# Layer 1: the q and k projections of images 2 to 7 as three one-pass products, with the blocks around the feed-forward in another order

## The chip, the cores and the metric

The kernel runs on one core of a Trainium2 chip. The metric is device time in microseconds (us) of one launch, weights and inputs in device memory; lower is better. TensorE (PE) multiplies matrices into PSUM, VectorE (DVE) and ScalarE (ACT) evict and transform, GpSimd (POOL) does small statistics, SyncE (SP) issues nearly all transfers.

## What is computed

The reference, cut to what matters, for 8 images of 384 channels and 32x32 = 1024 tokens:

```python
# layer 0
x = x + _L0_conv_ref(_gn(x), ...)            # group norm, 8-head attention with a relative bias
# layer 1
t = _to_tokens(x)
t = t + _L1_attn_ref(_ln_t(t), qkv_w, proj_w, proj_b)
t = t + _L1_ffn_ref(_ln_t(t), W1, b1, W2, b2)

def _L1_attn_ref(x, qkv_w, proj_w, proj_b):
    qkv = (x @ qkv_w.T).reshape(B, N, 3, H, D).transpose(2, 0, 3, 1, 4)   # H = 6, D = 64
    q, k, v = qkv[0], qkv[1], qkv[2]
    q, k = _normalize(q), _normalize(k)      # mean and deviation over the 64 of a head
    attn = softmax(q @ k.T * scale)
    return (attn @ v) ... @ proj_w.T + proj_b
```

The feed-forward has weights reduced to signs around a group mean and an 8-bit scale from the largest absolute value of an image; by its grouping only images 0 to 4 get one. Everything is float32.

## The kernel before, in words

The work is written out by hand in the order in which each engine is to do it (`tc.manual_schedule()`); nothing reorders it. Every engine works through its own list in order, and SP issues transfers in order, waiting at the head of its list for whatever the next transfer needs. `later.after(n, work)` puts work off by n calls of `later.step()`.

**Layer 0** (`_layer0`) goes image by image: 32 units of attention (`scores`, `weigh`), then the projections of the next image. Those of images 1 to 7 are already done in the manner that the change takes to layer 1: `cut_weights` (L511) cuts the weights into a high part (upper mantissa bits), a low part and a mix of both, stores them in device memory, and `Ahead.project` (L581) multiplies each part in one pass (type fp32r): high x high and low x low add up in one PSUM tile (`pg`), mixed x mixed fills a second (`pm`); ACT and DVE then combine the two into q or k. A block is one (pair of heads, q or k); there are six, and each is 18 matmuls of 128x512.

**Layer 1** (`_layer1`) goes image by image: 24 units of attention (`scores` L1486, `weigh` L1535), then the rest. Images 0 to 4 have a feed-forward, and there the six q/k projections of the next image (`project_qk`, L1342: six float32 matmuls, one PSUM tile, one DVE copy L1350 or L1352, one ACT square L1358) stand between its parts as work for PE while other engines are busy. The order around image b's feed-forward is: value projections 0, 1, 2 of the next image (`project_v`, L1423), between them the last two units' `weigh`; `project_out` (L1632, residual L1640); block 0 with the token sums in its middle (`token_sums` L1309); block 1; block 2; head sums of pair 0 (`head_sums` L1371); block 3; `feed_forward_1` (y1p, L1727) with the head sums of pair 1; block 4; block 5; value projection 3; `feed_forward_2` (y2p, L1778) with the head sums of pair 2.

Three chains run beside this. (1) The layer norm (`layer_norm`): token sums, `trf` copy, four small transfers and POOL steps, broadcasts `lc` and `ls`, then on DVE scale (L1671), shift (L1674), on ACT the cast to the high part (L1675), on DVE the low part `lun` (L1679), for three chunks k. (2) The normalisation of q and k (`normalise_qk`): a small transfer `hc`, a power on POOL (L1392), `hi`, `kc`, and some steps later the broadcasts `rq` and a DVE multiply (L1413). (3) The scale of the feed-forward: the maxima of the twelve y1 tiles on DVE (L1714), an all-reduce, `quant_scale`, then gelu (L1758), `hy` (L1766) and `ly` (L1767), which feed y2p.

Images 5 and 6 have no feed-forward; there `attention_inputs` does the six blocks, the head sums, and the four value projections in one go.

PSUM is one pool of four tiles of 128x1024 (`mm2`, tag "p"). A tile is handed on when the engine that reads it has passed that reading instruction. The pool "w" of layer 1 has 16 tiles of 128x1024 in SBUF.

Of the kernel before, what the change touches and what calls it, by code (L numbers as in the profile page):

```python
# [19 lines left out]
F32 = mybir.dt.float32  # L20
# [7 lines left out]
P = 128  # L28
# [72 lines left out]

class _Shared:
# [23 lines left out]
class _Weights:  # L126
# [4 lines left out]
    def __init__(self, tc, ins, ready, shared):  # L131
        self.nc, self.ins, self.ready, self.shared = tc.nc, ins, ready, shared

# [39 lines left out]
    def store(self):  # L173
        self.nc.sync.dma_start(self.ready, self.w.rearrange("p k c -> p (k c)"))

# [17 lines left out]
def _layer0(tc, ins, x1, sums, shared, weights, beside):  # L193
# [9 lines left out]
    with ExitStack() as ctx:  # L203
# [298 lines left out]
        blocks = [(pair, s) for pair in range(NF0) for s in range(2)]  # L502
        BB = len(blocks) // 2
        cut = dram.tile([len(blocks), P, 3, KC, P], F32, tag="cut", name="cut", bufs=1)

        def masked(out, of):

            nc.vector.tensor_single_scalar(
                out.bitcast(INT), of.bitcast(INT), MASK, op=ALU.bitwise_and
            )  # L510

        def cut_weights(k):


            w = plain[:, ts(k, 2 * C)]
            high, low = etile(f"ch{k}")[:, 0 : 2 * C], etile(f"cl{k}")[:, 0 : 2 * C]
            parts = [etile(f"c{i}_{k}", dtype=F32R)[:, 0 : 2 * C] for i in range(3)]
            masked(high, w)
            nc.scalar.copy(parts[0], high)
            nc.vector.tensor_sub(low, w, high)  # L520
            nc.vector.tensor_scalar_mul(parts[1], low, CUT)
            nc.vector.scalar_tensor_tensor(parts[2], low, -CUT, high, ALU.mult, ALU.add)
            for i, part in enumerate(parts):
                nc.sync.dma_start(
                    cut[:, :, i, k].rearrange("n p c -> p n c"),
                    part.bitcast(F32).rearrange("p (n c) -> p n c", c=P),
                )

        class Cut:


            def __init__(self):
                t = shared.pool.tile([P, KC * 3 * C], F32R, tag="w", name="wc")
                self.w = t.rearrange("p (n i k c) -> p n i k c", n=BB, i=3, k=KC)

            def load(self, n):
                pair, s = blocks[n]
                nc.sync.dma_start(
                    self.w[:, n % BB].rearrange("p i k c -> p (i k c)").bitcast(F32),
                    cut[s * NF0 + pair].rearrange("p i k c -> p (i k c)"),  # L540
                )

        class Ahead:
# [16 lines left out]
            def mask(self, k):  # L560
                masked(self.high(k), self.xn[:, k])
# [13 lines left out]
            def mixed(self, k):  # L575
                t = etile(f"xd{self.b}_{k}", dtype=F32R)
                nc.vector.scalar_tensor_tensor(
                    t, self.parts[1][k].bitcast(F32), -CUT, self.high(k), ALU.mult, ALU.add
                )
                self.parts[2].append(t)  # L580

            def project(self, weights, n):
                pair, s = blocks[n]
                t = self.tile(pair)[:, s]
                name = f"{self.b}_{pair}_{s}"
                ps = mm2("pg" + name), mm2("pm" + name)
                for i in range(3):
                    for k in range(KC):
                        for h in range(NH):
                            nc.tensor.matmul(  # L590
                                ps[i // 2][:, h], weights.w[:, n % BB, i, k],
                                self.parts[i][k][:, ts(h, HALF)],
                                start=(k == 0 and i != 1), stop=(k == KC - 1 and i != 0),
                            )
                by = D0**-0.5 if s == 0 else 1.0
                nc.scalar.activation(  # L596
                    t, flat2(ps[1]), AF.Identity, scale=-by / CUT,
                    bias=bq[:, pair : pair + 1] if s == 0 else bqk[:, s, pair : pair + 1],
                )
                nc.vector.scalar_tensor_tensor(  # L600
                    t, flat2(ps[0]), by * (1.0 + 1.0 / CUT), t, ALU.mult, ALU.add
                )
                last = self.tile(NF0)
                for j in range(2):
                    nc.sync.dma_start(
                        last[j * S0 + pair * FR : j * S0 + (pair + 1) * FR, s],
                        t[j * S0 + D0 : (j + 1) * S0],
                    )
                later.step()
# [194 lines left out]
        for k in range(KC):  # L804
            later.after(18 + 3 * k, lambda k=k: cut_weights(k))
        for b in range(B):
            held = []
            for i, u in enumerate(units):
# [15 lines left out]
                if i == 26 and b == 0:  # L824
                    weights_qk = Cut()
                    for n in range(BB):
                        weights_qk.load(n)
# [14 lines left out]
            order = [n % len(blocks) for n in range(b % 2 * BB, b % 2 * BB + len(blocks))]  # L842

            def project(some):
                for n in some:
                    ahead.project(weights_qk, n)
                    if n in order[:BB]:
                        weights_qk.load((n + BB) % len(blocks))
# [346 lines left out]
def _layer1(tc, ins, x1, out, shared, start, before=None, check=None):  # L1195
# [4 lines left out]
    with ExitStack() as ctx:  # L1200
# [14 lines left out]
        def wtile(name, shape=(P, N)):  # L1215
            return work.tile(list(shape), F32, tag="w", name=name)
# [42 lines left out]

        tiny = const.tile([P, 2], F32, tag="tiny", name="tiny")  # L1260
# [8 lines left out]
        v = const.tile([P, MT, C], F32, tag="v", name="v")  # L1269

# [94 lines left out]

        def head_sums(b, pair, sq, d):
# [51 lines left out]
        def project_v(b, xt, m2, c=None, copy=nc.vector.tensor_copy):  # L1418

            pv = mm2(f"pv{b}_{m2}")  # L1420
            for i in range(2):
                for k in range(KC):
# [3 lines left out]
                        wqkv[:, k, 2 * C : 3 * C], start=(k == 0), stop=(k == KC - 1),  # L1426
# [228 lines left out]
        def layer_norm(b, xt, c):  # L1655
# [30 lines left out]
            def finish():  # L1686
                for k in range(1, KC):
                    scaled(k)
                    low(k - 1)
                    shifted(k)  # L1690
                low(KC - 1)
# [125 lines left out]
        def attention_inputs(b, xt, rest=(), sums=None):  # L1817
# [12 lines left out]
            for pair in range(NP1):  # L1830
                for s in range(2):
                    project_qk(b, pair, s, xt, qk, sq)
                    if (pair, s) == (0, 1):
                        token_stats(f"a{b}", tk)
                    if s == 0 and pair > 0:
                        head(pair - 1, *((3, 3) if pair == 1 else (5, 4)))
            for work in rest:
                work()
                later.step()
# [12 lines left out]
        for name, weights, shape, at, totals, means, signs in (  # L1852
# [6 lines left out]
            for g in range(NG):  # L1859
                later.after(totals[g], lambda g=g, stages=stages: stages[1](g))  # L1860
                later.after(signs[g], lambda g=g, stages=stages: stages[3](g))
        later.after(1, rest_of_pools)
        qk, kc = attention_inputs(0, xt)
        behind = None
        for b in range(B):
# [9 lines left out]
            for i, u in enumerate(units):  # L1875
# [7 lines left out]
                if i == 3:  # L1883
# [5 lines left out]
                    if more:  # L1889
                        *ahead_sums, stages = fold(f"a{b + 1}", ahead)  # L1890
                        for at, stage in zip((13, 14, 15, 19, 20), stages):
                            later.after(at - i, stage)
            if not more:
# [6 lines left out]
            if not ffn:  # L1900

                def last(i, b=b, oT=oT, held=held):
# [5 lines left out]
                    b + 1, ahead, [lambda: last(0), lambda: last(1)], ahead_sums  # L1908
# [4 lines left out]
            else:  # L1913
                nqk, sq, d, nkc = {}, {}, head_rows(b + 1), kc_tile(b + 1)

                def project(pair, s, step=True, middle=None):
                    return project_qk(b + 1, pair, s, ahead, nqk, sq, step, middle)
# [4 lines left out]
                for i in range(2):  # L1922
                    project_v(b + 1, ahead, i)
                    weigh_last(b, oT, held[i])
                divide(b, oT, [NP1 - 1], (1, 1))
                project_v(b + 1, ahead, 2)
                fsq, fc = [], []
                project_out(b, oT, xt, lambda m, _: fsq.append(square(f"f{b}", xt, m)), later.step)
                two = wtile(f"two{b}")
                nc.vector.tensor_add(two, xt[:, 0], xt[:, 1])  # L1930
                nc.vector.tensor_add(fsq[0], fsq[0], fsq[1])
                project(
                    0, 0,
# [4 lines left out]
                )  # L1938
                tk = fc[1]
                un, begin, normal = layer_norm(b, xt, fc[0])  # L1940
                project(0, 1)
                take = project(1, 0, step=False)
# [4 lines left out]
                take = project(1, 1, step=False)  # L1947
                normal()
                take()

                def between_1(m):
                    if m == 2:
                        normalise(0, 5, 2)
                    elif m == 4:
                        head_sums(b + 1, 1, sq, d)
                        normalise(1, 5, 3)

                y1, top = feed_forward_1(b, un, between_1)
                project(2, 0)
# [3 lines left out]
                supply.gelu(1)  # L1963
                supply.split(0)
                project(2, 1, step=False)()
# [4 lines left out]
                def between_2(k):  # L1970
                    if k == 0:
# [12 lines left out]
def tile_conv_attn_hybrid(ctx: ExitStack, tc: tile.TileContext, ins, out):  # L1984
    dram = ctx.enter_context(tc.tile_pool(name="x1", bufs=1, space=DRAM))
    x1 = dram.tile([B, C, N], F32, tag="x1", name="x1")
    ready = dram.tile([P, KC * 3 * C], F32, tag="ready", name="ready")
    state = ctx.enter_context(tc.tile_pool(name="state", bufs=1))
    flag = state.tile([P, 1], mybir.dt.int32, tag="flag", name="flag")
    sums = state.tile([P, B, NP0, 2 * N // P], F32, tag="sums", name="sums")  # L1990
    with ExitStack() as main, tc.manual_schedule():
# [3 lines left out]
            tc, ins, x1, sums, shared, _Weights(tc, ins, ready, shared),  # L1995
# [3 lines left out]
            tc, ins, x1, out, shared, start, before,  # L1999
# [4 lines left out]
    with tc.If(out_of_range > 0):  # L2004
        _layer0_shifted(tc, ins, x1)
        with ExitStack() as again, tc.manual_schedule():
# [4 lines left out]
            _layer1(tc, ins, x1, out, shared, start)  # L2011
# [44 lines left out]
```

## Time and profile before

| what | value |
|---|---|
| device time, three runs | 3014.68, 3003.15, 3005.71 us; median 3005.71 |
| the profiled execution's own time | 3006.06 us |
| its span in the profile | 3004.1 us |
| mean granted PE clock | 0.999 |
| layer 0 / layer 1, by the start of layer 1's first sums | to 1402.6 us / from there |
| one image of layer 1 with a feed-forward (2, as an example) | 1912.3 to 2136.7 us |
| one image without | 2723.8 to 2878.0 us |

How to read it: the span is the time between the first and the last instruction in the trace. Busy shares are of that span. In the view of waits a row says which instruction of an engine waited for which other, us in total, times, and the longest. The timeline gives start, duration, engine, line and tile, and in brackets the idle time of that engine before the instruction with what ended it. A float32 matmul is recorded as two instructions.

### The profile page before, as it was taken

The page shows a single profiled execution, that of the slowest core. Times are in us where ns is not written, and L with a number is a line of the kernel's source. Part 1 is how long each engine was busy: PE and PEld are TensorE (multiplying, and loading weights), DVE is VectorE, ACT ScalarE, POOL GpSimd, SP SyncE. Part 2 cuts the span into 40 slices and gives each one's busy share as a digit, 9 for nine tenths or more (in the row PEclk, how much of TensorE's full clock was granted, in tenths as well). Part 3 has the DMA queues.
Part 4 walks back from the last instruction along what each step waited for, and adds up shares of the span by engine and source line. Part 5 has one row for each costly group of instructions (what it writes and reads, how often), then busy time and mean ns, then how long its engine had stood idle before and what let it go on. Part 6 is the DMA issues. An engine that isn't in the chain of part 4 may idle for free.

```text
span 3004.1 us, 46389 instructions
## 1 busy us (share of the span) xinstructions
PE 2974.7 (99%) x19154; PEld 1640.6 (55%) x19154; DVE 1871.5 (62%) x1861; ACT 1447.9 (48%) x1802; POOL 469.4 (16%) x315
## 2 busy tenths in 40 slices
PE   8999999999999999999999999999999999999999
PEld 3355656656565656644546656656656656645453
DVE  3775747575665747564655755755755755755546
ACT  2653626354553626353553643643644643654534
POOL 3120202121110202112202202202202202211110
PEclk9999999999999999999999999999999999999999
DMA  7533030312213030223301101101101101102011
GB/s 201 147 104 93 23 110 17 96 37 51 76 30 97 23 111 17 75 81 97 77 23 31 51 23 31 51 23 31 51 23 31 51 23 31 51 17 72 17 52 38
DMA packets 114285, 171.22 MB, mean 57 GB/s; under 512 B 60848, under 2 KB 71328, under 8 KB 113712
## 3 DMA queue, kind: packets, MB, share of 16 engines
q1 hardware_dynamic: 110800, 166.33, 19.3%
q8 instruction: 154, 2.52, 0.4%
q10 hardware_dynamic: 3264, 1.82, 0.2%
q14 instruction: 67, 0.55, 0.1%
HBM read 126.44 MB, written 32.61 MB: 53 GB/s over the span
## 4 chain that ended last, share of the span: by engine, by line
PE 90%; DVE 4%; DMA 3%; SPq 2%; ACT 1%; issue 1%; POOL 1%; DVEq 0%; ACTq 0%; POOLq 0%
PE o L673 14%; PE s L642 14%; PE s L1486 11%; PE o L1535 11%; PE y2p L1778 6%; PE pq L1342 5%; PE pp L737 4%; PE pv L1423 4%; PE y1p L1727 4%; PE pp L1632 4%; PE pg L590 4%; PE pv L616 4%; PE pm L590 2%; SPq L403 1%; DVE e L653 1%; PE sum L1562 1%
## 5 line engine op out<-in xcount | busy, mean ns | idle before, releaser
L653 DVE TENSOR_TENSOR e<-s,grow 128x1024 f32<-128x1024 f32 x512 | 600.9, 1217 | 167.8 <-PE s L642 167.5
L657 ACT ACTIVATE e<-e 128x1024 f32<-128x1024 f32 x512 | 535.6, 1057 | 337.9 <-DVE e L653 317.4
L642 PE MATMUL s<-qk 48*64 48x512 f32 x4096 | 610.6, 593 | 9.9 <-DVE e L653 9.4
L673 PE MATMUL o<-e,v 64*64 64x512 f32 x4096 | 603.7, 590 | 0.9 <-DVE e L653 0.9
L1497 ACT ACTIVATE e<-s,kc 128x512 f32<-128x512 f32 x768 | 463.9, 694 | 170.8 <-PE s L1486 160.3
L1486 PE MATMUL s<-qk,qk 64*64 64x512 f32 x3072 | 418.3, 592 | 0.3
L1535 PE MATMUL o<-e,v 64*64 64x512 f32 x3072 | 414.8, 590 | 0.0
L642 PEld LDWEIGHTS s<-qk 48*64 48x64 f32 x4096 | 234.9, 132 | 242.5 <-issue 93.7
L673 PEld LDWEIGHTS o<-e,v 64*64 64x64 f32 x4096 | 250.1, 133 | 189.8 <-issue 99.0
L1512 DVE TENSOR_TENSOR t<-t,e 128x1024 f32<-128x1024 f32 x192 | 230.9, 1221 | 54.0 <-ACT e L1497 53.9
L1486 PEld LDWEIGHTS s<-qk,qk 64*64 64x64 f32 x3072 | 153.5, 132 | 190.1 <-issue 109.5
L1342 PE MATMUL pq<-bx,wqkv 128*128 128x512 f32 x576 | 254.1, 595 | 0.7 <-ACT tra L1314 0.7
L1535 PEld LDWEIGHTS o<-e,v 64*64 64x64 f32 x3072 | 157.6, 133 | 171.1 <-issue 143.8
L702 POOL TENSOR_TENSOR inv<-sums,over 128x16 f32<-128x16 f32 x32 | 93.4, 2917 | 891.7 <-DMA sums<-sd 749.0
L1342 PEld LDWEIGHTS pq<-bx,wqkv 128*128 128x128 f32 x576 | 107.8, 190 | 143.5 <-issue 139.7
L1509 DVE TENSOR_TENSOR t<-e,e 128x1024 f32<-128x1024 f32 x96 | 114.2, 1224 | 81.5 <-ACT e L1497 81.4
L1714 DVE TENSOR_REDUCE parts<-y 128x1 f32<-128x1024 f32 x75 | 90.1, 1217 | 94.4 <-ACT y L1711 93.9
L1358 ACT ACTIVATE qsq<-pq 128x1024 f32<-128x1024 f32 x48 | 49.2, 1025 | 190.6 <-DVE qk L1352 101.9
L1392 POOL TENSOR_TENSOR hc<-hc,rsqrt 128x32 f32<-128x32 f32 x24 | 138.5, 5772 | 2.0
L1423 PE MATMUL pv<-wqkv,bx 128*128 128x384 f32 x384 | 131.9, 497 | 0.0
L600 DVE SCALAR_TENSOR_TENSOR qk<-pg,qk 128x1024 f32<-128x1024 f32 x42 | 51.4, 1225 | 128.2 <-ACT qk L596 128.2
L1423 PEld LDWEIGHTS pv<-wqkv,bx 128*128 128x128 f32 x384 | 119.1, 315 | 19.0 <-issue 9.7
(185 smaller groups left out, 3298.3 us busy)
## 6 DMA issues: line engine op xcount, KB each, us to landing
rb<-rd SPq DMA_DIRECT2D x110, 256.0 KB
wc<-cut SPq DMA_DIRECT2D x24, 576.0 KB
xn<-in_x_dram SPq DMA_DIRECT2D x24, 512.0 KB
res<-in_x_dram SPq DMA_DIRECT2D x24, 512.0 KB
x<-res SPq DMA_DIRECT2D x24, 512.0 KB
bx<-x SPq DMA_DIRECT2D x8, 1536.0 KB
rq<-hi SPq DMA_DIRECT2D x48, 256.0 KB
out_dram<-bx SPq DMA_DIRECT2D x23, 512.0 KB
```

The costliest lines, as they stand in the source:

```text
L590: nc.tensor.matmul(ps[i // 2][:, h], weights.w[:, n % BB, i, k], self.parts[i][k][:, ts(h, HALF)], start=(k == 0 and i != 1), stop=(k == K ...
L642: nc.tensor.matmul(s[j][ts(c, QP), i], qk[pair][rows, 1, ts(4 * m2 + 2 * i + c, QP)], qk[pair][rows, 0, ts(h, HALF)], start=True, stop=True,)
L653: nc.vector.tensor_add(e.rearrange("p (i q) -> p i q", i=2), s[j], bass.AP(near.tensor, near.offset, [near.ap[0], [-QROWS * IW, 2], [1, HA ...
L657: nc.scalar.activation(e, e, AF.Exp)
L673: nc.tensor.matmul(po[ts(j, S0), r], v[keys, 2 * m2 + i, 2 * pair + j, :], es[j][keys, ts(i, HALF)], start=(m2 == 0 and i == 0), stop=(m2 ...
L1342: nc.tensor.matmul(pq[:, h], wqkv[:, k, s * C + pair * P : s * C + (pair + 1) * P], xt[:, k, ts(h, HALF)], start=(k == 0), stop=(k == KC - 1),
L1423: nc.tensor.matmul(pv[:, i, 0:C], xt[:, k].rearrange("c (p m) -> c m p", m=MT)[:, 2 * m2 + i], wqkv[:, k, 2 * C : 3 * C], start=(k == 0), ...
L1486: nc.tensor.matmul(s[j][ts(c, QP), i], qk[pair, 1][rows, ts(4 * m2 + 2 * i + c, QP)], qk[pair, 0][rows, ts(h, HALF)], start=True, stop=True,)
L1497: nc.scalar.activation(e[:, ts(i, HALF)], s[j][:, i], AF.Exp, scale=kc[:, pair, j, m : m + 1])
L1512: nc.vector.tensor_add(total[j], total[j], e)
L1535: nc.tensor.matmul(po[ts(j, D1), r], v[keys, 2 * m2 + i, at : at + D1], es[j][keys, ts(i, HALF)], start=(m2 == 0 and i == 0), stop=(m2 == ...
L1778: nc.tensor.matmul(py[m][:, h], w2[:, k, ts(m, P)], supply.parts[k][i][:, ts(h, HALF)], start=(k == 0 and i == 0), stop=(k == FC - 1 and i ...
```

## The change

Layer 1 gets the cut products for images 2 to 7. The helpers of layer 0 move to the top of the file. The weights of layer 1 are cut during image 1 of layer 0 (units 17 to 26) and kept in device memory. Image 1 of layer 1 keeps the float32 products. For images 2 to 7 the high, low and mixed parts of the normalised input are made on DVE and ACT during the attention units of the image before and kept in the room of the feed-forward's second weight, `w2`, which is stored once and loaded again for each feed-forward. Weight blocks go through four slots; blocks 4 and 5 are loaded into the slots of 0 and 1. A block writes two PSUM tiles and its mixed product comes first, except for the first block of an image. Layer 0's blocks after the first of an image also take the mixed product first.

Around the feed-forward the order for b = 1 to 4 becomes: value projection 0; the last two `weigh`; block 0; `project_out`; block 1 with the token sums; blocks 2 and 3; head sums of pair 0; blocks 4 and 5; `feed_forward_1` with the head sums of pairs 1 and 2; value projections 1, 2, 3; `feed_forward_2`. The weight of the value projections has a tile of its own (`wv`).

The diff, cut to its core (helpers that only moved are left out):

```diff
+    def products(self, n, i, out, part):
+        w = self.slots[n % len(self.slots)].rearrange("p (i k c) -> p i k c", i=3, k=KC)
+        for k in range(KC):
+            for h in range(NH):
+                self.nc.tensor.matmul(
+                    out[:, h], w[:, i, k], part[k][:, ts(h, HALF)],
+                    start=(k == 0 and i != 1), stop=(k == KC - 1 and i != 0),
+                )
...
+                if b == 1 and i in (17, 20, 23):
+                    k = (i - 17) // 3
+                    t = etile(f"cw{k}")[:, 0 : 2 * C]
+                    weights.load_part(k, t)
+                    later.after(3, lambda k=k, t=t: weights.cut(k, t, *cut_tiles(f"1{k}")))
...
-                    ahead.project(weights_qk, n)
+                    ahead.project(cuts, n, (0, 1, 2) if n == order[0] else (2, 0, 1))
...
+        def project_cut(b, n, parts, dst, sq, step=True, middle=None, order=(2, 0, 1)):
+            pair, s = BLOCKS[n]
+            name = f"{b}_{pair}_{s}"
+            ps = mm2("pg" + name), mm2("pm" + name)
+            for at, i in enumerate(order):
+                if middle is not None and at == 2:
+                    middle()
+                cuts.products(n, i, ps[i // 2], (parts.high, parts.low, parts.mixed)[i])
+            def take():
+                t = qkp.tile([P, N], F32, tag="qk", name="qk" + name)
+                to = t if s == 0 else t.rearrange("c (m p) -> c p m", m=MT)
...
+                nc.scalar.activation(to, of[1], AF.Identity, scale=-1.0 / CUT)
+                nc.vector.scalar_tensor_tensor(to, of[0], 1.0 + 1.0 / CUT, to, ALU.mult, ALU.add)
+                q = wtile("qsq" + name)
+                nc.scalar.activation(
+                    q if s == 0 else q.rearrange("c (p m) -> c p m", m=MT), to, AF.Square
+                )
...
+                        cuts.load(0)
+                        cuts.load(1)
+                        parts = Parts(b + 1, ahead)
+                        for k, at in enumerate((8, 10, 12)):
+                            later.after(at - i, lambda k=k, parts=parts: parts.cut_high(k))
+                        for k, at in enumerate((16, 17, 18)[: 1 if ffn else KC]):
+                            later.after(at - i, lambda k=k, parts=parts: parts.cut_low(k))
+                        for k, at in enumerate(() if ffn else (19, 21, 22)):
+                            later.after(at - i, lambda k=k, parts=parts: parts.mix(k))
...
+                else:
+                    project_v(b + 1, ahead, 0)
+                    weigh_last(b, oT, held[0])
+                    for k in range(1, KC):
+                        parts.cut_low(k)
+                    weigh_last(b, oT, held[1])
+                    divide(b, oT, [NP1 - 1], (1, 1))
+                    for k in range(KC):
+                        parts.mix(k)
+                    project(0, order=(0, 1, 2))
                 fsq, fc = [], []
                 project_out(b, oT, xt, lambda m, _: fsq.append(square(f"f{b}", xt, m)), later.step)
+                if b > 0:
+                    cuts.load(4)
...
                 tk = fc[1]
                 un, begin, normal = layer_norm(b, xt, fc[0])
-                project(0, 1)
-                take = project(1, 0, step=False)
+                project(first_now + 1)
+                take = project(first_now + 2, step=False)
                 begin()
                 take()
                 later.step()
                 head_sums(b + 1, 0, sq, d)
...
+                    take = project(4, step=False)
+                    normal(1)
+                    take()
+                    take = project(5, step=False)
+                    normal(2)
+                    take()
+                    normal(3)
+                    w2 = load_w2(b)

                 def between_1(m):
                     if m == 2:
                         normalise(0, 5, 2)
                     elif m == 4:
                         head_sums(b + 1, 1, sq, d)
                         normalise(1, 5, 3)
+                    elif m == 6 and b > 0:
+                        head_sums(b + 1, 2, sq, d)
+                        normalise(2, 5, 3)

                 y1, top = feed_forward_1(b, un, between_1)
-                project(2, 0)
+                if b == 0:
+                    project(4)
+                else:
+                    project_v(b + 1, ahead, 1, copy=nc.scalar.copy)
```

In `attention_inputs` (images 6 and 7) the six `project_qk` become six `project_cut`; the last two `weigh` and the sum of the last pair move from behind the six blocks to behind block 0, and the first normalisation's steps go from (3, 3) to (3, 2).

## The prediction

> **What bounds the kernel.** First the page and the view of what PE waits for.
>
> ```profile
> PE 2974.7 (99%) x19154; PEld 1640.6 (55%) x19154; DVE 1871.5 (62%) x1861; ACT 1447.9 (48%) x1802; POOL 469.4 (16%) x315
> ```
> ```profile
> PE s L642 <- DVE e L653: 9.4, 5, 2.5
> ...
> PE y1p L1727 <- ACT qsq L1358: 1.9, 5, 0.4
> ```
>
> PE is busy for all but 29 us, and nearly all of those lie before 200 us. So a PE microsecond taken out counts in full, and each new wait of PE is added in full. The last line matters: after the layer norm PE already waits 0.4 us per image for a PSUM tile whose eviction stands behind layer-norm work. The chain of waits in order of time shows what hides there, from the token sums of image 1 (they start on PE at 1805.75) on:
>
> ```profile
> 1808.05 0.59 ACT trf L1314
> ...
> 1815.42 1.58 DMA lr<-tcf
> ...
> 1817.07 3.98 DMA lc<-lr
> ...
> 1821.07 1.22 DVE un L1671
> ...
> 1822.38 1.23 DVE un L1674
> ```
>
> The broadcast arrives 15.3 us after the sums start, the first chunk is shifted at 17.9, and its cast ends at 18.9. PE meanwhile does 21.9 us of work and starts y1p at 1827.65: everything just fits. Second, the timelines of SP and DVE in the same image:
>
> ```profile
> 1844.56 0.59 SPq L1377 DMA_DIRECT2D hd<-hr  x1
> 1846.34 0.32 SPq L1390 DMA_DIRECT2D hc<-hd  x1
> 1853.89 0.33 SPq L1393 DMA_DIRECT2D hi<-hc  x1
> 1855.31 1.25 SPq L1395 DMA_DIRECT2D kc<-hi  x2
> 1856.60 2.59 SPq L1406 DMA_DIRECT2D rq<-hi  x4
> ```
> ```profile
> 1861.90 1.23 DVE L1413 TENSOR_TENSOR qk<-qk,rq 128x1024 f32<-128x1024 f32 x1 [1.58 <-DMA rq<-hi]
> ```
>
> One normalisation holds SP for 12.0 us (1844.56 to 1856.56), most of it waiting for POOL's power (5.42 us). The broadcast lands 5.3 us after its issue, and DVE waits for it at the head of its list.
>
> **What is saved.** The price of a block stands in the chain, float32 for image 6, one-pass in layer 0:
>
> ```profile
> 2685.63 10.50 PE pq L1342 x24
> ```
> ```profile
> 380.61 2.79 PE pg L590 x12
> 384.80 2.79 PE pg L590 x12
> ```
>
> Two float32 blocks take 10.50 us (10.30 without a head sum), so one 5.2; a one-pass block starts every 4.19 (18 matmuls of 0.233). Saved: 1.0 a block, 6.1 an image, 36 us for 36 blocks. [...] The trace's 0.233 holds over the 42 blocks of layer 0, so the sum goes by the row.
>
> **First new wait: the layer norm, images 1 to 4.** The built order says what each instruction waits for. Blocks are 0 to 5 in order; each holds two of the four PSUM tiles, `pm` until an ACT copy, `pg` until a DVE operation behind it. The tile for `pg` of block 4 comes free with the ACT copy of block 3, and on ACT that copy stands behind the layer norm's first cast, since `begin()` is issued before `take()`. Time from the start of the token sums:
> - PE reaches block 4's `pg` after sums 2.98 (1805.75 to 1808.73), rest of block 1 1.40, blocks 2 and 3 8.38, head sums 0.98, `pm` 1.40: 15.1.
> - The cast ends at 18.9 (unchanged chain), the ACT copy (1.12, row L596) at 20.1. PE waits 5.0, and leaves block 5 at 27.1.
> - DVE then does block 3's operation (1.94, the strided copy L1352), three layer-norm operations at 1.14, ACT the second cast 1.05 and block 4's copy: 27.7, which y1p's first tile needs (wait 0.6). Block 4's DVE operation ends at 28.9 (wait 0.3).
> - Three more layer-norm operations, the third cast (33.4) and block 5's copy, 34.6: y1p's third tile needs that one. PE, done with two first parts at 29.8, waits 4.8.
> Sum 10.7 an image. The work that covers it is the same as before (19 us of blocks); what is gone is its freedom to run ahead, since two blocks now fill PSUM where one copy freed a tile. [...]
> Not in the trace: ACT copy and square with a stride, for k. Bounds 1.02 to 1.94 (DVE's contiguous and strided rows reach 1.22 and 1.94; ACT's contiguous is the nearest); I take 1.12. At 1.94 it adds 0.8 twice, 1.6 an image. The load of block 5's weights stands on SP before `lr`, and waits for block 1 on PE; that ends at 4.4, before `tca` is even issued (6.8): 0 to 1 us, I take 0.
>
> **Second new wait: the quantising scale, images 1 to 4.** Pair 2's normalisation now stands on SP before the `rq` of pair 0, whose DVE multiply stands before the last two maxima. From the end of pair 1's head sums: `hd` 0.75, pair 1 done on SP 12.75, pair 2 done another 12.0 later (24.8), `rq` landed 5.3 later (30.1). Then multiply 1.15, two maxima 2.4, last maximum 0.25, second multiply 1.15, scale 0.5, gelu 1.15, `hy` 0.7: 37.5. PE in that time: seven groups of y1p at 2.8, head sums 1.0, three value projections at 3.87: 32.2. Wait 5.3, and 0.6 more for `ly`: 5.9. Before, that broadcast landed at 1861.9 and y2p did not wait. If pair 1's part is less late the price falls to 0 at worst for this forecast; if POOL is slowed as in its 6.3 us rows it is 1.8 more.
>
> **Smaller terms.** Block 0's mixed part comes 0.3 late from DVE. `project_out` needs the last pair's division; from the sums' end to its DVE multiply 12.8 before (1783.6 to 1796.4), against 4.5 of block 0 and 10.3 of products ahead of it: covered with 2 to spare. An image with a feed-forward thus costs 10.7 + 5.9 + 0.3 - 6.1 = +10.8; four, **+43**.
>
> Images 6 and 7: blocks saved 6.1. Evictions (ACT 2.1, DVE 1.2 to 1.9 a block) stay inside 4.19, and nothing slow stands between them. But pair 0's `rq` still lands 30.7 after its head sums (2685.56 to 2716.30), and PE now needs only 30.3 from there to the next scores (three blocks, two head sums, 15.8 of value projections); with the multiply and a value scaling behind it PE waits 2.6. So -3.5 each, **-7**.
>
> Layer 0: in image 0 the three weight cuts (3.0 us of DVE each) cost PE 6.4 us of waits (2.5, 1.9, 2.0, between 140 and 182 us). Three more in image 1: **+6**; bounds 3 (DVE idles 1.1 per unit there) and 10 (units wait for the stores too). With the mixed product first, the last block's DVE operation no longer waits for ACT (414.76 now, 413.6 then), and the next unit's additions start 0.6 earlier in seven images: **-4**, bounds -6 and 0.
>
> Costed at nothing: masks, casts and low parts in the units (of a unit's 3.44 us ACT's exponentials need 2.42 and DVE's two additions 2.4; uncovered, DVE's 0.68 + 1.22 + 1.22 and ACT's 1.04 for three chunks are up to 12 us an image); the store and loads of `w2` (2.36 MB, 6 us at the 400 GB/s seen with `wc`, 50 us before y2p; the load waits on SP for block 5, and pair 0's `hc` behind it becomes some 8 us late, which still ends before pair 1's `hd`); weight blocks (0.58 MB, loaded tens of us ahead); `wv` (1.5 us beside the first products).
>
> Sum: 43 - 7 + 6 - 4 = +38. The profiled execution took 3006.06 (span 3004.1), 0.35 above the median of 3005.71: **3044**.
>
> **Rivals.**
> - *Only the layer-norm wait.* SP gets to pair 2 early enough, the second wait is gone: 38 - 24 = +14, 3020. For it: the second wait's terms are long and each has play. Against: SP and POOL work in order, and 12.0 is measured with one pair only. Chance 0.20, half of it within 0.5%.
> - *Faster: the PSUM waits don't bind.* Place: block 4's `pg` and y1p's third tile. If block 3 is evicted before the layer norm's first cast, PE runs on, and the saving of 36 is kept less 6 for the cuts and 2.6 twice: about 3006 - 36 + 6 - 4 + 5 = 2977. It decides at 5.0 us: the chain to the cast must be that much shorter than 18.9, or the tile must come from another release. For it: PE before had the same cover and waited 0.4. Against: the chain is of fixed transfers, and the order on ACT is written in the built program. Chance 0.12.
> - *It does not do what it says*: excluded, the built order has the 36 blocks with 18 matmuls each.
>
> **Numbers.** Both waits, as worked out: 0.68, 3044, alone 3026 to 3066 (strided ACT, slow POOL, 10 for the cuts above; shorter second wait below). The range takes in most of the first rival: 3012 to 3066. Something below 0.5% (15 us) can't be told from no change: faster 0.12, same 0.10 (half the first rival), slower 0.78.
>
> **What would show it.** Right: PE waits at y1p and in block 4 for ACT, of about 5 us, four times each; y2p waits for `hy` by 5; `rq` issued after pair 2's `kc`; a block every 4.19. Wrong: no idle PE between the token sums and y1p's third tile; the cast ending long before 18.9; new waits inside the attention units; a block price other than 4.2.

## The result: slower by 3.1%, and the profile after

The changed kernel takes 3102.76 us (median of 4 runs, 3102.30 to 3103.86), the kernel before, beside it, 3009.96 (4 runs, 3003.15 to 3014.68): a ratio of 1.031 with a 95% interval of 1.029 to 1.034. The forecast was 3044 with a range to 3066. The direction was right; the size was not: +38 forecast, +93 measured, +97.7 between the two profiled spans (3004.1 and 3101.8).

The page of the changed kernel, first its line for PE, then the granted clock of TensorE in 40 slices of the span:

```profile
PE 2987.9 (96%) x19370; PEld 1696.0 (55%) x19370; DVE 1929.4 (62%) x1919; ACT 1539.6 (50%) x1861; POOL 496.4 (16%) x315
...
PEclk9999999999999999999999999999998999999999
```

PE was to lose 36 us of work, yet its busy time rose by 13. One slice shows an 8, and the run's mean clock is 0.983 (0.999 before). Next what PE waits for (us in all, times, longest):

```profile
PE y2p L1891 <- DVE hy L1879: 22.1, 4, 6.3
PE pg L149 <- ACT qk L1463: 22.0, 4, 6.6
PE s L660 <- DVE e L671: 20.3, 9, 4.1
PE y1p L1840 <- ACT qk L1463: 15.6, 4, 4.3
PE ph L423 <- DMA w<-in_L_conv_mlp_w_dram: 8.1, 2, 7.8
PE s L1597 <- ACT e L1608: 8.0, 6, 2.2
PE s L1597 <- DVE qk L1524: 6.4, 2, 3.3
```

The first, second and fourth line are the forecast's new waits, four times each, 5.5 + 5.5 + 3.9 us an image. The chain of waits in time shows the first of them as it was worked out, from the token sums (1826.28) on:

```profile
1826.28 1.92 PE tsf L1352 x16
...
1835.62 1.59 DMA lr<-tcf
...
1837.27 4.18 DMA lc<-lr
...
1844.06 1.04 ACT un L1786
1845.11 1.80 ACT qk L1463
```

The cast ends 18.8 us after the sums' start (18.9 forecast), and block 3's copy stands behind it. SP's timeline and DVE's show the second:

```profile
1890.56 0.60 SPq L1488 DMA_DIRECT2D hd<-hr  x1
1892.33 0.32 SPq L1501 DMA_DIRECT2D hc<-hd  x1
1901.23 0.33 SPq L1504 DMA_DIRECT2D hi<-hc  x1
1902.64 1.25 SPq L1506 DMA_DIRECT2D kc<-hi  x2
1903.99 2.55 SPq L1517 DMA_DIRECT2D rq<-hi  x4
```
```profile
1909.01 1.23 DVE L1524 TENSOR_TENSOR qk<-qk,rq 128x1024 f32<-128x1024 f32 x1 [13.49 <-DMA rq<-hi]
```

So the waits are there, and of the forecast length. What is new is what stands behind each. PE's timeline (start, duration, instruction) around y1p's third tile:

```profile
1856.64 0.63 PE L1840 MATMUL y1p<-un,w 128*128 128x512 f32 x2
1857.11 0.63 PE L1840 MATMUL y1p<-lun,w 128*128 128x512 f32 x2
1861.85 1.22 PE L1840 MATMUL y1p<-un,w 128*128 128x512 f32 x2 [4.11 <-ACT qk L1463]
1862.87 1.05 PE L1840 MATMUL y1p<-lun,w 128*128 128x512 f32 x2
...
1866.28 1.05 PE L1840 MATMUL y1p<-lun,w 128*128 128x512 f32 x2
1867.13 0.89 PE L1840 MATMUL y1p<-un,w 128*128 128x512 f32 x2
1867.87 0.62 PE L1840 MATMUL y1p<-lun,w 128*128 128x512 f32 x2
```

Such a pair of matmul records starts 0.47 us after the one before it ahead of the wait, and 0.85 to 1.0 us after it for some six us behind the wait. Windows cut at these places show why; the number behind POOL's count is the granted clock:

```profile
1851.00:1858.00 7.00, 6.73 (x29) 5.09 (x28) 4.96 (x6) 3.49 (x4) 0.00 (x0) 1.00 0.30 87
1858.00:1868.00 10.00, 6.15 (x15) 4.85 (x16) 3.99 (x3) 4.87 (x3) 4.05 (x2) 0.66 0.43 180
1868.00:1876.00 8.00, 8.00 (x37) 6.47 (x36) 4.24 (x4) 4.25 (x4) 2.48 (x1) 1.00 0.03 3
```

The trace's record of the granted clock has 20 stretches at half speed between 80 us and the last microseconds, granted 0.50, each 3.41 or 6.83 us long, all beginning in a wait or up to 2 us behind one (before: 2). Half of PE's busy time in them is lost: 45.0 us against 3.4. The difference of the spans comes apart by stage, from the windows' ends, PE's idle time, and this record:

| stage | forecast | span | idle PE | half clock | PE's work |
|---|---|---|---|---|---|
| layer 0, image 0 | 0 | +7.9 | +1.9 | +6.5 | -0.5 |
| layer 0, image 1's cuts | +6 | +12.4 | +8.1 | +2.8 | +1.5 |
| layer 0, order of products, 7 images | -4 | -2.9 | -0.4 | 0 | -2.5 |
| layer 1, images 1 to 4 | +43 | +73.3 | +65.9 | +28.9 | -21.5 |
| layer 1, images 5 to 7 | -7 | +6.3 | +9.6 | +3.4 | -6.7 |
| start, layer 1's image 0 | 0 | +0.6 | -0.6 | 0 | +1.2 |

### The profile page after: what moved, and what is told of

Its sections match the earlier page's. It is cut to its first block, busy times and chain, and to the rows that moved or that the text cites. A ratio compares the mean times of both kernels' runs of the same rounds, so it can differ in the third digit from the quotient of the medians.

```text
span 3101.8 us, 47033 instructions
## 1 busy us (share of the span) xinstructions
PE 2987.9 (96%) x19370; PEld 1696.0 (55%) x19370; DVE 1929.4 (62%) x1919; ACT 1539.6 (50%) x1861; POOL 496.4 (16%) x315
## 4 chain that ended last, share of the span: by engine, by line
PE 78%; DMA 7%; DVE 5%; POOL 3%; ACT 3%; issue 3%; SPq 1%; DVEq 0%; POOLq 0%; ACTq 0%
PE s L660 13%; PE o L691 13%; PE s L1597 10%; PE o L1646 9%; PE y2p L1891 6%; PE pg L149 5%; PE pp L755 4%; PE pv L634 4%; PE pp L1743 3%; PE y1p L1840 3%; PE pm L149 2%; POOL hc L1503 2%; PE pv L1534 2%; PE pq L1385 1%; ACT e L1608 1%
## 5 line engine op out<-in xcount | busy, mean ns | idle before, releaser
L660 PE MATMUL s<-qk 48*64 48x512 f32 x4096 | 618.8, 598 | 20.4 <-DVE e L671 20.3
L691 PE MATMUL o<-e,v 64*64 64x512 f32 x4096 | 612.8, 594 | 0.0
L1597 PE MATMUL s<-qk,qk 64*64 64x512 f32 x3072 | 438.0, 598 | 16.7 <-ACT e L1608 8.0
L1646 PE MATMUL o<-e,v 64*64 64x512 f32 x3072 | 426.0, 591 | 0.0
L1891 PE MATMUL y2p<-hy,w 128*128 128x512 f32 x360 | 118.7, 412 | 22.1 <-DVE hy L1879 22.1
L1840 PE MATMUL y1p<-un,w 128*128 128x512 f32 x360 | 119.1, 413 | 15.9 <-ACT qk L1463 15.6
L634 PE MATMUL pv<-wv,xn 128*128 128x384 f32 x384 | 128.9, 490 | 0.0
L1534 PE MATMUL pv<-wv,bx 128*128 128x384 f32 x384 | 128.3, 491 | 0.0
L1743 PE MATMUL pp<-oT,L_attn_proj_wT 128*128 128x512 f32 x288 | 126.0, 594 | 0.8 <-DVE oT L1709 0.8
L755 PE MATMUL pp<-oT,wp 128*128 128x512 f32 x288 | 125.7, 595 | 0.0
```

The source lines that it names most:

```text
L634: nc.tensor.matmul(pv[:, i, 0:C], xn[:, k, ts(2 * m2 + i, P)], wv[:, k, :], start=(k == 0), stop=(k == KC - 1),)
L660: nc.tensor.matmul(s[j][ts(c, QP), i], qk[pair][rows, 1, ts(4 * m2 + 2 * i + c, QP)], qk[pair][rows, 0, ts(h, HALF)], start=True, stop=True,)
L691: nc.tensor.matmul(po[ts(j, S0), r], v[keys, 2 * m2 + i, 2 * pair + j, :], es[j][keys, ts(i, HALF)], start=(m2 == 0 and i == 0), stop=(m2 ...
L755: nc.tensor.matmul(pps[b, m][:, h], (wp[:, k] if k < NF0 else wl)[:, ts(m, P)], oT[:, k, ts(h, HALF)], start=(k == 0), stop=(k == (NF0 if ...
L1597: nc.tensor.matmul(s[j][ts(c, QP), i], qk[pair, 1][rows, ts(4 * m2 + 2 * i + c, QP)], qk[pair, 0][rows, ts(h, HALF)], start=True, stop=True,)
L1646: nc.tensor.matmul(po[ts(j, D1), r], v[keys, 2 * m2 + i, at : at + D1], es[j][keys, ts(i, HALF)], start=(m2 == 0 and i == 0), stop=(m2 == ...
```

## The experiments

Two theories stood against each other. **G**: a wait costs its length, and behind it some microseconds at half the clock. **R**: the slow matmuls belong to the changed blocks (contention, the weights' reload), and a wait costs its length. "Before" is the kernel before, run beside each (medians 3007.0 to 3008.3).

**The waits filled** (`e1_fill`). Block 4's mixed product four times, sixteen throwaway matmuls in y1p's second tile, half of a value projection three times:

```diff
-                cuts.products(n, i, ps[i // 2], ...)
+                for _ in range(4 if n == 4 and i == 2 and b - 1 < NG else 1):
+                    cuts.products(n, i, ps[i // 2], ...)
...
-            for i in range(2):
+            for i in (0, 0, 0, 1) if again else range(2):
```

> The changed kernel with PE kept busy in its three new waits of images 1 to 4 by products done again, whose results are overwritten by the same values: the mixed product of block 4 four times instead of once (3 x 1.4 us), sixteen matmuls into the second y1p tile before its real ones (3.7 us), and the first half of the last value projection three times (3.9 us). Nothing of what PE waits for comes earlier; only the idle time is filled. Theory G (a wait costs its length and, behind it, some microseconds at half the clock): the granted clock stays at full speed in these places and the time falls by about the 27 us that the half clock costs there (per image 5.9 to 7.6), to some 3076, less where the filling is longer than the wait (up to 1 us an image): 3074 to 3082. Rival R (the slow matmuls behind the waits belong to the changed blocks themselves, by contention with w2 or by the cut weights, and not to the idle time): the time stays at 3103 or rises by a few us.

Measured 3088.84, 14 us faster than the change with 51 us more matmul time. PE's waits in the same places:

```profile
PE y2p L1899 <- DVE hy L1887: 7.9, 4, 3.3
...
PE y1p L1848 <- ACT qk L1464: 5.8, 4, 1.5
PE pg L149 <- ACT qk L1464: 5.0, 4, 1.6
```

In images 1 to 4 the loss to half clock fell from 28.9 to 6.2. The filling was longer than the waits it replaced (12.7 us for 9.8 an image), which is why 14 came out and not 27, outside the range that G was given; but R, which has no gain at all here, falls.

**A wait put into the kernel before** (`e5_wait`), in front of `largest` in `feed_forward_1`:

```diff
+            for _ in range(7):
+                nc.vector.tensor_reduce(parts[:, FC - 1 : FC], y1[FC - 1], AX.X, ALU.max, ...)
```

> The kernel before, with nothing of the change, and one wait put in: the last maximum of the first feed-forward product is taken eight times instead of once (7 x 1.22 = 8.5 us on DVE) in images 0 to 4, so that hy comes later. hy was 3.1 us ahead of y2p, so PE should wait 5.4 us, five times. Theory G: each wait is followed by some 2.4 us of loss at half the clock, 5 x 7.8 = +39. Rival R (a wait costs its length): +27.

Measured 3042.88: +35.8. What PE waits for at y2p:

```profile
PE y2p L1782 <- DVE hy L1770: 13.6, 5, 3.0
...
PE y2p L1782 <- ACT qsq L1358: 3.9, 5, 1.3
PE y2p L1782 <- DVE ly L1771: 2.7, 5, 0.5
```

PE idles 4.2 us more in each of the five images (2.65 to 2.97 in one piece), 21.1 in all, and loses 14.0 to half clock; images 0 to 4 are 37.9 longer in this profile. By its length alone the wait would have cost 21, and even the fastest execution is 28 slower than the slowest of the kernel before. Layer 1 has none of the change's blocks here, so the loss belongs to the wait.

**The second wait undone** (`e3_scale`):

```diff
-                    elif m == 6 and b > 0:
-                        head_sums(b + 1, 2, sq, d)
-                        normalise(2, 5, 3)
...
-                    if k == 0 and b == 0:
+                    if k == 0:
```

> The changed kernel with pair 2's head sums and normalisation of images 2 to 5 put back to the start of the second feed-forward product, so that SP issues pair 0's rq before them. The prediction's second new wait should vanish: y2p no longer waits for hy (22.1 us in four images), and with it the 10.0 us of half clock behind it: 3103 - 32 = 3071 by theory G, 3103 - 22 = 3081 if a wait costs only its length. If pair 2 then comes too late for the next scores, up to 5 us an image come back there.

Measured 3063.95, -38.8. The line of y2p is gone from PE's waits. Between the two profiles images 1 to 4 are 33.6 us shorter, as G has it: 21.4 of idle time, 11.1 of half clock. (Layer 0's image 0, which this edit does not touch, is 7.7 shorter in this profile as well.)

**Evictions ahead of the layer norm as well** (`e7_evict`):

```diff
-                begin()
-                take()
+                take()
+                begin()
...
-                    normal(1)
-                    take()
+                    take()
+                    normal(1)
```

> The run with pair 2's normalisation put back (3064), and the evictions of blocks 3, 4 and 5 issued ahead of the layer-norm work of the same place instead of behind it. Theory of the first wait (block 4's tile comes late because the copy of block 3 stands behind the layer norm's cast on ACT): the wait at block 4's pg, 5.2 to 6.3 us, goes. But DVE then reaches the layer norm's later chunks some 3 us later, and y1p waits for these instead: by the durations on record about 6 us in place of 9.5 an image, in pieces of 1 to 3, so with little half clock: 3064 - 4 x (3.5 + 3) = 3038. If the first wait has another cause (the transfers of the statistics), it stays: 3060 to 3068.

Measured 3046.59, another -17 (-26 expected). PE's waits:

```profile
PE y1p L1840 <- DVE lun L1790: 11.0, 10, 2.0
PE y1p L1840 <- ACT qk L1463: 9.4, 4, 2.3
...
PE pg L149 <- ACT hr L1487: 4.5, 4, 1.3
```

Block 4's wait went from 5.6 to 1.1, so the order on ACT was its cause. The rest moved to y1p, 5.1 us an image in pieces of 0.5 to 2.3, for DVE's low parts and ACT's copies: as expected, the layer norm and the evictions do not both fit beside the shorter blocks.

**Layer 0 alone** (`e4_layer0`), every use of the one-pass blocks in layer 1 replaced by the old branch:

```diff
-                    if more and b > 0:
+                    if more and b > B:
...
-                    if b == 0:
+                    if parts is None:
```

> Layer 0 of the changed kernel alone (three weight cuts in image 1, mixed product first), with layer 1 in float32 blocks in the old order. By the trace of the changed kernel layer 0 ends some 18 us later than before, of which 7.9 lie in image 0, whose program the change hardly touches, and 12.4 in image 1 (8.1 idle, 2.8 half clock, the rest in the units); the order of products gives 2.9 back. If image 0's part belongs to the change: 3010 + 18 = 3028. If it is a matter of the single run: about 3010 + 9.5 = 3020. The prediction had +6 - 4: 3012.

Measured 3022.13, +15. Image 1, from its first scores to the next image's, takes 182.7 us (169.1 before; where an expectation below speaks of 150.7 and 141.7, it counts some 27 us less of it). Image 0 takes 171.3. The same image 0 takes 169.0 in the kernel before and 173.1 in the one with the wait put in, which leaves layer 0 as it was; in the five traces with the change's image 0 it takes 169.2 to 176.9. What of the 7.9 us belongs to the change stays open; 6.5 of them are half clock.

**Each cut spread over four units** (`e6_spread`):

```diff
-                later.after(3, lambda k=k, t=t: weights.cut(k, t, *cut_tiles(f"1{k}")))
+                for j, step in enumerate(weights.cut(...)):   # mask, subtract, mix, scale
+                    later.after(3 + j, step)
```

> Layer 0 of the changed kernel with layer 1 in float32, as in the run of layer 0 alone (3022), but with each weight cut spread over four units, one DVE operation (0.7 to 0.8 us) in each, in images 0 and 1, instead of four in one unit. DVE idles about 1.1 us in a unit, so if the stalls come from four operations in one place, the three waits of image 1 (8.1 us, 4.3 of half clock) go, and most of those of image 0 with them: 3022 - 12 = 3010 or less; with image 0 quiet too, about 3000, which is below the kernel before. If the stalls come from DVE having no time in these units at all, or from the stores, they stay: 3018 to 3022.

Measured 3013.19: 9 us better, but image 1 still takes 179.8. Operations of 0.6 to 1.0 us in every unit stall it too, in smaller pieces (6.0 us of idle PE in place of 8.2); the expectation was missed.

**Three together** (`e8_move`): the above, a value projection moved, masks earlier, `rq` of images 6 and 7 earlier.

```diff
                 head_sums(b + 1, 0, sq, d)
+                if b > 0:
+                    project_v(b + 1, ahead, 1, copy=nc.scalar.copy)
...
+                    low(1)
+                    scaled(2)
+                    project(5, step=False)()
+                    shifted(2)
```

> All three together, for a version that keeps what the one-pass blocks save: pair 2's normalisation back, weight cuts spread, evictions ahead of the layer-norm work, a value projection (3.9 us of PE) moved from behind y1p to before block 4, the masks two units earlier, and in images 6 and 7 pair 0's rq issued before pair 1's normalisation. If waits and the half clock behind them are all that was lost: blocks save 5.6 in each of six images, waits of 1 to 2 us are left in four, the order in layer 0 gives 2.9: 3007 - 34 + 8 - 3 = 2978, with the units' 1.8 us an image 2985. If the moved projection only moves the wait to y2p (7.9 us of products then cover the quantising chain, which needs about 7 to 8), 3000 to 3010.

Measured 3019.42 (2978 to 2985 expected), a miss. The three waits are gone but for 2.2 us at y1p, y2p does not wait; but images 1 to 4 still take 225.3 to 227.5, and PE's waits name what is left:

```profile
PE s L1615 <- ACT e L1626: 16.2, 14, 2.1
PE s L675 <- DVE e L686: 14.1, 9, 2.6
```

The units wait for ACT's exponentials, beside which the copies of the masked chunks stand on ACT, and layer 0's cuts remain.

**Images 6 and 7 alone** (`e9_tail`), `more and b >= NG`, and:

```diff
-                    head(pair - 1, *((3, 3 if parts is None else 2) if pair == 1 else (5, 4)))
+                    head(pair - 1, *((1, 4) if pair == 1 else (5, 4)))   # with parts
```

> One-pass blocks in images 6 and 7 alone (images 2 to 5 in float32 as before), weight cuts spread, and pair 0's rq issued before pair 1's normalisation. The wait of 3.2 us before the scores of images 6 and 7 and its 1.7 of half clock should go: each image keeps 5.6 of blocks less 1.8 in the units. Against the run with spread cuts alone: -7 to -11. If rq comes no earlier, -0 to +3.

Measured 3010.79, 2.4 below the spread cuts alone, which ten executions of each, some 10 us apart among themselves, do not tell from nothing. The wait for `rq` is gone; in the profile 2.2 us an image are left of the saving, and PE waits for the units' exponentials once an image (1.2 us).

**Cuts in layer 1's first feed-forward** (`e10_late`), and the same with **the copies on POOL** (`e11_pool`); images 6 and 7 alone with those cuts (`e12_tail`):

```diff
+                def between_1(m):
+                    if b == 0:
+                        for op in cut_ops[3 * m : 3 * m + 3]:   # 256 columns each
+                            op()
```
```diff
-                nc.scalar.copy(self.high[k], t)
+                nc.gpsimd.tensor_copy(self.high[k], t)
```

> The combined version (3019), with the weights of layer 1 cut in layer 1's first feed-forward, nine pieces of 256 columns, three short DVE operations per group of y1p in image 0, where DVE idles some 1.5 us per group, instead of in the units of layer 0's image 1. If those units' stalls were the cuts' whole price there, image 1 of layer 0 goes from 150.7 back to 141.7 and nothing comes in its place: 3019 - 9 = 3010, level with the kernel before. If the pieces hold up y1p or the quantising scale of image 0, 3012 to 3020.

> The same, and the copy of each masked chunk (1.0 us on ACT, three an image, beside the exponentials of the attention units) put on POOL, which idles there. In the units of images 1 to 6 PE waits for ACT's exponential twice, 1.17 and 1.18 us, and once more in images 1 and 3. If the copies are the cause, 2 to 3 us an image go in six images: 3010 - 14 = 2996. If POOL and DVE hinder one another, the units' additions on DVE become slower and the time rises above the other run's.

> One-pass blocks in images 6 and 7 alone, with the weights cut in layer 1's first feed-forward: the run of images 6 and 7 alone (3011) less the 9.7 us that layer 0's image 1 still lost there: 3001, below the kernel before by 0.2%, which is less than the 0.5% that can be told from no change.

Measured 3035.44, 3008.83 and 3026.41. All three have one wait of 22 us at y2p of image 0. DVE's waits in the POOL version, from 1610 to 1690 us, and SP's timeline show where it comes from:

```profile
DVE wt L128 <- DMA there<-wt: 18.0, 7, 11.9
DVE wt L107 <- DMA there<-wt: 11.0, 2, 9.2
```
```profile
1637.00 0.33 SPq L1511 DMA_DIRECT2D hc<-hd  x1
1644.45 0.33 SPq L1514 DMA_DIRECT2D hi<-hc  x1
1645.87 1.26 SPq L1516 DMA_DIRECT2D kc<-hi  x2
1647.23 5.25 SPq L118 DMA_DIRECT2D there<-wt  x5
```

The pieces' stores stand on SP behind a normalisation, and DVE behind the stores: the mechanism of the second wait once more, made by the experiment. POOL's copies themselves gave more than the 14 expected, 26.6: no unit waits for an exponential any more (16.7 us in 14 waits with the copies on ACT), so the copies on ACT were the cause, and images 1 to 4 took 221.1 to 223.4.

**Without that wait** (`e13_best`): the same, with the cuts in layer 0's images 2 to 4.

```diff
+                if 2 <= b <= 4 and i in (8, 14, 20):
+                    k, s = b - 2, (i - 8) // 6
+                    piece = etile(f"piece{k}{s}")
+                    weights.load_columns(k, s, piece[:, 0 : 2 * P])
+                    for j, step in enumerate(weights.cut_columns(k, s, piece)):
+                        later.after(2 + j // 2, step)
```

> The version with POOL's copies (3009), without the one wait it had left, 22.1 us at y2p of image 0 and 2.3 of half clock behind it: there DVE waited 29 us for the cut weights' stores, which stand on SP behind a normalisation. The weights of layer 1 are cut here in layer 0's images 2 to 4 instead, nine pieces of 256 columns, two short operations (0.3 and 0.4 us) a unit in eighteen units, where SP has no such wait. If the stores were the cause: 3009 - 24 = 2985, and 2985 to 2992 if the units lose some tenths; that is 0.5 to 0.8% below the kernel before (3008). If layer 0's units have no room for even such short operations: 2 us for each of the nine pieces, about 3003.

Measured 2982.90 (ratio to before 0.9915, interval 0.990 to 0.993): 0.85% faster than the kernel before and 3.9% faster than the change. Its page and waits of PE:

```profile
PE 2941.0 (99%) x19370; PEld 1680.0 (56%) x19370; DVE 1938.6 (65%) x1943; ACT 1521.8 (51%) x1843; POOL 488.5 (16%) x333
```
```profile
PE s L682 <- DVE e L693: 9.1, 6, 3.2
...
PE y1p L1863 <- ACT un L1809: 4.4, 4, 1.1
PE y1p L1863 <- ACT qk L1486: 2.2, 4, 0.6
PE y1p L1863 <- DVE lun L1813: 2.1, 4, 0.5
```

The same 19370 matmul records as in the change, 47 us less PE busy time: nearly all of what the change spent there was half clock (45.0 us, 3.4 here), not matmuls. Layer 0's units had room for operations of 0.3 to 0.4 us: their scores wait 9.1 us for DVE, 9.4 in the kernel before.

## Why the prediction was wrong

- **The failed step: "each new wait of PE is added in full".** It gave a wait the price of its length. The twelve waits of 3.5 to 6.6 us each cost a further 1.6 to 2.9 at half clock: 27.2 us behind them, 28.9 in images 1 to 4 and 41.7 in the whole span, most of the missing 55 to 60 (6.5 of the 41.7 lie in layer 0's image 0, where the cause stays open). The trace of before showed it: behind layer 0's wait of 2.55 us, one of those from which the prediction took the price of the cuts, eleven scores take 2.83 us, behind the next one of 2.46 they take 1.51 (PE's timeline; the granted clock from 148 to 153 us is 0.66).

```profile
145.50 0.59 PE L642 MATMUL s<-qk 48*64 48x512 f32 x1
148.64 2.83 PE L642 MATMUL s<-qk 48*64 48x512 f32 x11 [2.55 <-DVE e L653]
150.41 1.06 PE L673 MATMUL o<-e,v 64*64 64x512 f32 x1
...
163.27 1.51 PE L642 MATMUL s<-qk 48*64 48x512 f32 x11 [2.46 <-DVE e L653]
```

- *First new wait*: right, by its mechanism and its place. 4.9 to 6.6 at `pg` (5.0), 3.5 to 4.3 at y1p's third tile (4.8), 9.4 an image on average (10.7; the small waits of 0.6 and 0.3 did not show). The strided copy took 1.88 us here (1.80 of it in the chain above), near its upper bound of 1.94, not 1.12. That the third tile's wait still came out near is partly luck: in image 1 the copy it needs ended 35.6 us after the sums' start (34.6 worked out), but PE, slowed by the half clock behind the first wait, got there at 31.5 (29.8).
- *Second new wait*: right. 5.0 to 6.3 (5.3); the 0.6 for `ly` did not show.
- *Block price*: nearly. A block starts every 4.30 (4.19 forecast), first and last lines here from image 6; PE's work fell by 5.1 to 5.7 an image (6.1).

```profile
2771.99 1.21 PE L149 MATMUL pm<-pw,wc 128*128 128x512 f32 x4
...
2776.29 1.10 PE L149 MATMUL pm<-pw,wc 128*128 128x512 f32 x4
```

- *Images 6 and 7*: wrong in sign. The wait for `rq` was 3.2 (2.6), but 1.7 of half clock came behind it, and from the first to the last scores images 5 and 6 took 2.8 and 5.8 us longer than before (1.7 of the latter is that half clock).
- *Costed at nothing, the work in the units*: not nothing. With the copies on ACT the scores of images 2 to 4 took 1.8 to 2.6 us longer, those of image 1 5.4, 1.7 of it half clock; with the copies on POOL images 2 and 4 are back at the 80.8 us of before. The other zeros held: no wait names `w2`, the weight blocks or `wv`.
- *Layer 0*: the cuts in image 1 cost 12.4, above the upper bound of 10, of which 2.8 are half clock. The order of products gave 2.9 (4). The waits of image 0 from which the price was taken are 2.5, 2.5 and 1.4, not 2.5, 1.9 and 2.0; their sum of 6.4 is right. Of the 29 us in which PE is not busy before, 19 lie before 200 us and 7 behind PE's last matmul, so "nearly all before 200" was misread; that PE bounds what lies between is untouched.
- *Rivals*: the case of the layer-norm wait alone (3020) had the second wait gone; it came, and the run without it still takes 3064. The faster case needed block 4's tile to come free before the cast. In the change it did not; in the last experiment, with the evictions ahead of the cast and the waits covered, it did, at 2983 (2977 for the rival; that the two are close is chance, since that run also has a value projection moved, copies on POOL and the cuts elsewhere).

## What to carry to other kernels

Before pricing a new wait of TensorE, look at the matmuls behind an old one: if they run at half speed, a wait costs more than its length. Here twelve waits of 3.5 to 6.6 us, 59.7 in all, cost another 27.2, and idling was dearer than work that is thrown away: 51 us of repeated products made the changed kernel 14 us faster. When a product becomes shorter, ask which engine's queue was hidden behind it, and move evictions ahead of, and spare work in front of, what comes late. Put small operations, and the DMAs they issue, where their engine and its queue are known to be free.

## What the runs showed of the hardware

In these traces the half clock goes with idle time, not with a kind of matmul: of the same 19370 matmul records the changed kernel lost 45.0 us to it, the last version 3.4. Over the fourteen traces, from 100 us on, with waits of 0.2 us and more, those less than 3.5 us apart taken together and sorted by the longest of them:

| longest wait, us | groups | followed by half clock | mean loss |
|---|---|---|---|
| under 1.0 | 122 | 0 | |
| 1.0 to 1.6 | 91 | 9 | 1.7 |
| 1.6 to 3.0 | 62 | 40 | 2.2 |
| 3.0 and more | 41 | 41 | 2.2 |

The nine are all pairs of y1p's waits, 1.6 us together. In every trace all stretches at half speed begin a whole number of 3.41 us apart, as if on a grid (in the changed kernel's the first from 80 us on, at 82.53, and the last before the end, at 2973.62, are 847 steps of 3.413 apart). Cut on this grid, a window at full speed in which PE idled 2.0 us or more was followed by half speed in 64 of 64 cases (19 of 19 in the traces of the kernel before and of the changed one), one with 1.4 to 2.0 us in 26 of 65 (2 of 11 in those two), and one with less never (0 of 1665 in those two). In these runs, then, half speed went with how much of a wait fell into one window: in the trace of before the wait from 146.09 to 148.64 lies in one but for its last 0.1 us and is followed by half clock, the one from 160.81 to 163.27, which the grid cuts at 162.22, is not.

In the changed kernel ACT's copy of 128x1024 from PSUM took 1.00 to 1.03 us contiguous (for q) and 1.88 to 2.02 with a stride (for k); DVE's operation behind it 1.22 to 1.23 and 1.93 to 2.01. POOL's copy of a 128x1024 chunk took 1.14 and 1.23 on average in two runs, and DVE's additions in the same units 1.25 instead of 1.22 us.
